# A two-layer image kernel on one core: the next image's transposes in one block, a mask built on GpSimd, a norm spread over three rows

## The chip, the cores and the metric

The kernel runs on one core of one Trainium2 chip. The metric is the device time of one execution in microseconds (us). In the traces PE is TensorE (PEld its weight loads), DVE is VectorE, ACT is ScalarE, POOL is GpSimd, and SP issues most DMAs.

## The reference: two residual layers on 32 images

The input is `x` of 32 images of 56 x 56 tokens with 128 channels, in fp32. Each layer normalises its input over 32 groups of channels and adds its result to it:

```python
x = x + L0(_gn(x), ...)   # shifted-window attention: windows of 7 x 7, shift 3, 4 heads
x = x + L1(_gn(x), ...)   # Fourier layer, then a feed-forward of 512
```

Layer 0 rolls the image by 3, cuts it into 8 x 8 windows of 49 tokens, computes q, k and v, adds to the scores a table of relative positions and a mask of -100 between tokens that were not neighbours before the roll, takes the softmax, and projects. The mask differs from zero only in the last row and the last column of windows. Layer 1 takes a cosine transform along each axis, keeps 32 modes, mixes the channels for each mode, transforms back, sums the two axes, and applies `relu(h @ W1 + b1) @ W2 + b2`.

## The kernel before

Work goes by **rows of windows**: 7 lines of an image, 8 windows. An image has 8 rows (`NWR`), and one turn of the main loop (line 1006), a *cycle*, does one row of attention and, some cycles behind, a share of the Fourier layer of an earlier image. The order of the instructions on PE, ACT, DVE and POOL is written by hand (`manual_schedule`, line 999): each of these engines works in program order. Slots of a tile's buffers are given out by a planner when the kernel is built. What lies ahead of line 999 (constants, masks) is ordered by that planner too.

**A cycle** from the 12th on (`CONV_BEGIN` = 11) sorts its matmuls by the part of the PE array that they use: `halves_first` (q and k, line 371; the first matmul of the feed-forward, line 738), for cycles without feed-forward `half_columns` (forward transforms, line 627, and mixing, line 670), then `eighths` (attention times values of three rows ago, line 487), `quarters` (scores, line 417, and the transforms back, line 706), `full` (transposes that use the whole array) and `halves_last` (v, line 400, the rest of the transforms, the feed-forward's second matmul, line 766, and the projection, line 534). Six names are used below: `attn_max` (line 445) is DVE's maximum and POOL's subtraction, `attn_exp` (line 453) ACT's exponential, `attn_divide` (line 457) DVE's sum and reciprocal and POOL's multiplication (called mult), `attn_transpose` (line 467) PE's transposes of the softmax, whose first half is copied out by DVE and second half by ACT (aT), and `attn_sums` (line 557) two DVE reductions and an ACT square for the second layer's norm, of which `fourier_stats` (line 579) makes the scale and shift.

**The first eleven cycles** run `first_rows` (line 956), which has attention alone.

**The next image.** `image_groups(im, i)` (line 267) turns rows i and i + 1 of an image into channels x tokens: 7 PE transposes into two PSUM banks (line 275), three ACT copies into `xw` (lines 287, 288 and 293), two POOL memsets, two DVE `bn_stats` (line 297), and on POOL the projection's bias added to `x` (line 306, two instructions). PSUM has eight banks of one tile each: four called pa (`attn_bank`) and four called pc (`conv_bank`). `next_groups` (line 916) calls it twice in row 5 and twice in row 6 of the image before (the first image: rows 4 and 5). `full` does the softmax's transposes only in even cycles, for two rows at once. `image_norm` (line 315) is a generator in steps: the DVE chain and POOL's power (lines 333 to 355), the scaled weights `wn` and the negated mean `nb` (lines 359 and 362), and a small PE product for v's bias (line 365). For the first image all steps run before row 0; for the second in row 6, one after another; for later ones in row 7.

**The mask.** `bias_and_mask(r)` (line 187) adds the table of positions and the mask into `bm` with 16 instructions of 49 x 98; r = 0 is for the rows 0 to 6 and is done before the rows begin, r = 1 for row 7, done on DVE at the end of row 1 (line 985). Its source `mask_sb` lies in the buffer of the tag sq, which `attn_sums` uses from row 4 on.

Which cycle has no feed-forward: cycles 11 to 18, and later every row 6 (`FF_AT`, line 43). The transforms back stand in the Fourier cycles 5 to 8 (`back_groups`, line 829), which are the cycles 16 to 19 for the first image and have feed-forward beside them for nearly all others.

Of the kernel before, what the change touches and what calls it, by code (L numbers as in the profile page):

```python
# [10 lines left out]
F32 = mybir.dt.float32  # L11
# [4 lines left out]
P = 128  # L16
# [32 lines left out]
def swin_fourier_kernel(  # L49
# [33 lines left out]
    def attn_bank():  # L83
        return bank("pa", 4)
# [87 lines left out]
            )  # L172
    nc.sync.dma_start(rpb[JP : JP + WT], rpb[0:WT])

    mask_sb = work.tile([P, 4, C], F32, tag="sq", name="mask", bufs=1).rearrange("p n c -> p (n c)")
    mask_sb = mask_sb[:, : 4 * WT].rearrange("p (r k j) -> p r k j", r=2, k=2)
    nc.vector.memset(mask_sb, 0.0)
    for hh in range(2):
# [5 lines left out]
    nc.gpsimd.memset(bm, 0.0)  # L184
    rpb_f = rpb.rearrange("p (t u) y x -> p t u (y x)", u=2)

    def bias_and_mask(r):
        for t in range(2):
            for half in range(2):
                rows = slice(half * JP, half * JP + WT)  # L190
                for k, p0, p1 in ((0, 0, NP - half), (1, NP - half, NP)):
                    for p in range(p0, p1):
                        nc.vector.tensor_tensor(
                            bm[rows, r, t, p],
                            rpb_f[rows, t],
                            mask_sb[rows, r, k].unsqueeze(1).to_broadcast([WT, 2, WT]),
                            ALU.add,
                        )

    bias_and_mask(0)  # L200
# [66 lines left out]
    def image_groups(im, i):  # L267


        pt = [attn_bank(), attn_bank()]  # L270
        pts = [
            p[:, : n * S].rearrange("p (j r s) -> p j r s", r=n, s=WS) for p, n in zip(pt, (8, 6))
        ]
        for c in range(7):
            nc.tensor.transpose(  # L275
                pts[c // 4][:, :, 2 * (c % 4) : 2 * (c % 4) + 2],
                im.x[:, WS * i // 2 + c],
                ident_x[:, :, SS:].rearrange("p r (j s) -> p j r s", s=WS),
            )
# [35 lines left out]
    def image_norm(im):  # L315
# [38 lines left out]
        rstd = small.tile([P, 1], F32, tag="rstd0", name="rstd0")  # L354
        nc.gpsimd.tensor_tensor(rstd, ve, mhalf, ALU.pow)
        im.w = work.tile([P, 3 * C], F32, tag="wn", name="wn")
        yield
        nb = small.tile([P, 1], F32, tag="nb0", name="nb0")
        nc.vector.scalar_tensor_tensor(
# [3 lines left out]
        yield  # L363
        pb = attn_bank()
        halved(pb[:, 0:1], wqkv[:, 2 * C :], nb)
        im.bias = small.tile([P, 5], F32, tag="bqkv", name="bqkv")
        nc.vector.tensor_copy(im.bias[:, 2:3], pb[:, 0:1])
        yield

# [451 lines left out]
    def row(r):  # L821
        return (images[r // NWR], r % NWR) if 0 <= r < NB * NWR else (None, 0)
# [17 lines left out]
    def nothing():  # L840
        while True:
            yield

    def load_first(cycle):
        for im, c in fourier(cycle):
            if c == 0:
                load_columns(im, 0)
                load_columns(im, 1)

    def halves_first(cycle, norm):  # L850
        for im, c in fourier(cycle):
            if c == 0:
                im.stats = fourier_stats(im)
                im.cols = {}
                next(im.stats)
        last, j = row(cycle - 4)
        sums = attn_sums(last, j) if last and cycle > CONV_BEGIN else nothing()
        next(sums)
        im, i = row(cycle)
        if im:  # L860
            attn_qk(im, i, False)
        next(norm)
        next(sums)
        for im, c in fourier(cycle):
            if c in FF_AT:
                ff_in(im, FF_AT.index(c))
        for im, c in fourier(cycle):
            if c == 0:
                next(im.stats)
# [21 lines left out]
                    mix(im, True, g)  # L891

    def quarters(cycle):
        im, i = row(cycle)
        if im:
            attn_scores(im, i, cycle)
        for im, c in fourier(cycle):
            for width, g in back_groups(c):
                modes_back(im, width, g)

    def eighths(cycle):
        im, i = row(cycle - 3)
# [13 lines left out]
    def next_groups(cycle):  # L916
        b, i = divmod(cycle, NWR)
        if b + 1 < NB:
            for j in {(4 if b == 0 else 5): (0, 2), (5 if b == 0 else 6): (4, 6)}.get(i, ()):
                image_groups(images[b + 1], j)  # L920

    def last_out(cycle):
# [4 lines left out]
    def halves_last(cycle, norm):  # L927
        im, i = row(cycle)
        if im:
            attn_v(im, i, cycle)  # L930
        if has_ff(cycle):
            half_columns(cycle)
        half_columns(cycle, True)
        load_back(cycle + 1)
        next_begin(cycle)
        load_first(cycle)
        next(norm)
        if row(cycle)[0]:
# [6 lines left out]
        next(norm)  # L945

    def next_begin(cycle):
        b, i = divmod(cycle, NWR)
# [7 lines left out]
    def first_rows(cycle, norm):  # L956
# [15 lines left out]
            attn_max(cycle)  # L972
        if im3:
            attn_project(im3, i3)
        next(norm)
        last, j = row(cycle - 4)
        if last:
            for _ in attn_sums(last, j):
# [7 lines left out]
        next(norm)  # L986
# [9 lines left out]
        next(norm)  # L996

    ET = mybir.EngineType
    with tc.manual_schedule(engines={ET.PE, ET.Activation, ET.DVE, ET.Pool}):
        images[0] = image_begin(0)  # L1000
        for i in range(0, NWR, 2):
            image_groups(images[0], i)
        for _ in image_norm(images[0]):
            pass
        norm = nothing()
        for cycle in range(NB * NWR + CONV_BEGIN + FF_AT[-1] - NWR + 1):
            if cycle < CONV_BEGIN:
                first_rows(cycle, norm)
            else:
# [10 lines left out]
                    half_columns(cycle)  # L1020
                eighths(cycle)
                quarters(cycle)
                if row(cycle)[0] and cycle % 2:
# [4 lines left out]
            norm = nothing()  # L1028
            if i == (NWR - 2 if b else NWR - 3) and b + 1 < NB:
                norm = image_norm(images[b + 1])  # L1030
                next(norm)


# [60 lines left out]
```

## Time and profile before

| | us |
|---|---|
| median of 3 runs | 3635.16 (3634.94 to 3637.57) |
| profiled execution | 3641.7 |
| its span, first to last instruction | 3639.9 |
| PE busy in the span | 3574.4 |
| DVE, ACT, POOL busy | 2211.9, 2148.1, 1368.3 |
| longest group: second feed-forward matmul (L112, pc<-wff,hid) | 740.3 for 12544, 273 ns each |
| transposes of L275 | 896, of 112x112 |
| POOL's subtract and multiply (L449, L463) | 389.4 and 389.1, 1521 and 1520 ns each |

A line of a timeline reads: start and duration in us from the span's start, engine, source line, operation, written tile <- read tiles, shape, count of merged instructions, and in brackets how long the engine was idle before and what ended that. Since matmuls overlap, the cost of a group on PE is read from its start to the start of the next group. The granted clock is the share of TensorE's full clock that the throttle allowed.

### The profile page before, as it was taken

What the parts mean: (1) busy time and instruction counts of PE and PEld (TensorE: products, weight loads), DVE (VectorE), ACT (ScalarE), POOL (GpSimd) and SP (SyncE); (2) the same over time, 40 slices, a digit from 0 to 9 for tenths busy, and PEclk for the clock granted to TensorE, in tenths of its full rate; (3) what the DMA queues carried; (4) which work ended last, traced back from release to release, by engine and by line L of the source; (5) the groups of instructions that cost most, each with busy time, mean ns of one, the idle gap of its engine ahead of it and who ended that gap; (6) DMA issues with size and microseconds to landing.
All of it is one profiled execution on the core that took longest, in us unless ns stands there. A gap on an engine that the chain in (4) does not pass through costs nothing.

```text
span 3639.9 us, 161666 instructions
## 1 busy us (share of the span) xinstructions
PE 3574.4 (98%) x72192; PEld 2832.6 (78%) x72192; DVE 2211.9 (61%) x4738; ACT 2148.1 (59%) x4044; POOL 1368.3 (38%) x1421
## 2 busy tenths in 40 slices
PE   7899999999999999999999999999999999999999
PEld 5677777778777787877777878777777777787776
DVE  7766666666666666666656656666566666565641
ACT  4555566655566555666556665556665556655553
POOL 5433333333343433333333434333333334343321
PEclk8999999999999999999999999999999999999999
DMA  4334434444434444334444344443444443444343
GB/s 114 86 102 112 113 96 111 108 110 111 112 97 112 112 109 116 94 110 107 113 108 111 94 114 109 113 114 94 111 108 111 110 111 94 114 109 109 97 115 98
DMA packets 687350, 390.31 MB, mean 107 GB/s; under 512 B 39967, under 2 KB 657600, under 8 KB 686400
## 3 DMA queue, kind: packets, MB, share of 16 engines
q1 hardware_dynamic: 686045, 379.65, 38.3%
q8 instruction: 568, 9.31, 1.1%
q14 instruction: 126, 1.03, 0.1%
q10 hardware_dynamic: 611, 0.32, 0.0%
HBM read 218.29 MB, written 161.48 MB: 104 GB/s over the span
## 4 chain that ended last, share of the span: by engine, by line
PE 92%; DVE 4%; issue 1%; ACT 1%; POOL 1%; DMA 1%; SPq 0%; POOLq 0%; DVEq 0%; ACTq 0%
PE pc L112 37%; PE pa L112 14%; PE pa L408 6%; PE pc L679 6%; PE pa L474 6%; PE pc L645 6%; PE pa L430 5%; PE pa L499 4%; PE pc L718 4%; PE pa L275 3%; DVE a L438 1%; DVE xf L729 0%; DVE oT L530 0%; POOL rstd L616 0%; ACT a L455 0%
## 5 line engine op out<-in xcount | busy, mean ns | idle before, releaser
L449 POOL TENSOR_TENSOR a<-a,mx 128x784 f32<-128x784 f32 x256 | 389.4, 1521 | 1427.3 <-DVE mx L448 1203.4
L112 PE MATMUL pc<-wff,hid 128*64 128x128 f32 x12544 | 740.3, 273 | 1.5 <-ACT hid L763 0.8
L112 PE MATMUL pc<-xf,wff 128*64 128x512 f32 (+2 forms) x3584 | 717.5, 539 | 1.1 <-DVE xf L729 1.0
L112 PEld LDWEIGHTS pc<-wff,hid 128*64 128x64 f32 x12544 | 702.6, 137 | 8.2 <-ACT hid L763 4.5
L460 DVE TENSOR_REDUCE sm<-a 128x16 f32<-128x784 f32 x256 | 248.2, 970 | 686.1 <-ACT a L455 682.8
L463 POOL TENSOR_TENSOR a<-a,rs 128x784 f32<-128x784 f32 x256 | 389.1, 1520 | 566.6 <-DVE rs L462 542.8
L763 ACT ACTIVATE hid<-pc,b1sb 128x512 f32<-128x512 f32 (+2 forms) x896 | 527.1, 632 | 76.6 <-PE pc L112 74.5
L112 PEld LDWEIGHTS pc<-xf,wff 128*64 128x64 f32 x3584 | 279.8, 137 | 368.0 <-issue 260.5
L379 ACT ACTIVATE q<-pa,bqkv 128x392 f32<-128x392 f32 x256 | 150.4, 587 | 473.1 <-PE pa L112 467.5
L112 PE MATMUL pa<-xw,wn 128*64 128x392 f32 (+1 forms) x2048 | 390.6, 497 | 3.7 <-DVE aT L484 2.7
L530 DVE TENSOR_SCALAR oT<-pa,bqkv 128x98 f32<-128x98 f32 (+2 forms) x768 | 171.0, 278 | 268.7 <-PE pa L499 268.6
L751 POOL TENSOR_TENSOR res<-res,b2sb 128x512 f32<-128x512 f32 (+2 forms) x256 | 264.2, 1037 | 113.5 <-DMA res<-scr 113.5
L408 PE MATMUL pa<-wn,xw 128*64 128x128 f32 x4096 | 283.6, 280 | 4.7 <-issue 3.5
L306 POOL TENSOR_TENSOR xl<-xl,bproj 112x512 f32<-112x512 f32 (+1 forms) x256 | 286.8, 1142 | 0.0
L499 PEld LDWEIGHTS pa<-aT,v 49*32 49x32 f32 x16384 | 172.9, 106 | 146.1 <-issue 127.0
L415 ACT COPY v<-pa 128x512 f32<-128x512 f32 x256 | 150.9, 589 | 228.3 <-PE pa L408 228.3
L438 DVE TENSOR_TENSOR a<-pa,bm 128x392 f32<-128x392 f32 x512 | 264.8, 559 | 25.8 <-PE pa L430 2.1
L455 ACT ACTIVATE a<-a 128x784 f32<-128x784 f32 x256 | 222.3, 869 | 97.2 <-POOL a L449 96.8
L482 ACT COPY aT<-pa 113x452 f32<-113x452 f32 x256 | 139.4, 544 | 210.4 <-PE pa L474 206.6
L408 PEld LDWEIGHTS pa<-wn,xw 128*64 128x64 f32 x4096 | 221.4, 137 | 38.6 <-issue 9.1
L112 PE MATMUL pa<-wproj,oT 128*64 128x128 f32 (+1 forms) x3584 | 248.0, 274 | 1.8 <-DVE oT L530 1.8
L448 DVE TENSOR_REDUCE mx<-a 128x16 f32<-128x784 f32 x256 | 246.3, 962 | 4.3
(91 smaller groups left out, 5583.8 us busy)
## 6 DMA issues: line engine op xcount, KB each, us to landing
zscr<-z SPq DMA_DIRECT2D x512, 112.0 KB
htok<-scr SPq DMA_DIRECT2D x256, 196.0 KB
zT<-zscr SPq DMA_DIRECT2D x192, 256.0 KB
res<-scr SPq DMA_DIRECT2D x160, 256.0 KB
out_dram<-res SPq DMA_DIRECT2D x160, 256.0 KB
scr<-xl SPq DMA_DIRECT2D x128, 224.0 KB
xl<-in_x_dram SPq DMA_DIRECT2D x32, 784.0 KB
xl<-in_x_dram SPq DMA_DIRECT2D x32, 672.0 KB
```

The lines of the kernel that those rows point to most:

```text
L112: nc.tensor.matmul(dst[ps], lhsT=lhsT[:, ps], rhs=rhs, start=start, stop=stop)
L306: nc.gpsimd.tensor_tensor(piece, piece, bproj.unsqueeze(1).to_broadcast([TC, e - a, C]), ALU.add)
L408: nc.tensor.matmul(pv[hs, j * C : (j + 1) * C], lhsT=im.xw[i][:, w * WT : w * WT + JP], rhs=im.w[:, 2 * C : 3 * C], start=True, stop=True,)
L438: nc.vector.tensor_tensor(a[:, 2 * hp : 2 * hp + 2, :, 0:WT].rearrange("p u w j -> p w u j"), ps[hp][:, :RT].rearrange("p (w u j) -> p w u ...
L448: nc.vector.tensor_reduce(mx, a3, axis=AX.X, op=ALU.max)
L449: nc.gpsimd.tensor_tensor(a3, a3, mx.unsqueeze(2).to_broadcast([P, 2 * NWR, WT]), ALU.subtract)
L455: nc.scalar.activation(a3, a3, AF.Exp)
L460: nc.vector.tensor_reduce(sm, a3, axis=AX.X, op=ALU.add)
L463: nc.gpsimd.tensor_tensor(a3, a3, rs.unsqueeze(2).to_broadcast([P, 2 * NWR, WT]), ALU.mult)
L499: nc.tensor.matmul(po4[u][h * HD : (h + 1) * HD, 2 * f + e], lhsT=v[ks, 2 * f + e, h * HD : (h + 1) * HD], rhs=im.aT[i][f][ks, h, e * JP : ...
L751: nc.gpsimd.tensor_tensor(res[:m, c0:c1], res[:m, c0:c1], b2sb[:m].unsqueeze(1).to_broadcast([m, c1 - c0, C]), ALU.add,)
L763: nc.scalar.activation(hf[:, :n], ph[:, :n], AF.Relu, bias=b1sb[:, f : f + 1])
```

## The change

- `next_groups`: from the second image on, all four calls for the next image stand in row 6, and row 5 has none. For the first image nothing moves.
- `image_groups`: the calls for i = 2 and 6 take their two PSUM banks from pc instead of pa.
- The mask: `mask_sb` moves to the tag res (first used by the feed-forward in cycle 19). `bias_and_mask` takes the engine and does a quarter of the work at a call; the table for row 7 is built on GpSimd, half (8 instructions) in cycle 4 and half in cycle 5, ahead of that cycle's `next_groups`.
- The norm: the generator goes on over cycles instead of being thrown away at the end of each. The first image's runs up to `wn` before row 0, and its small product comes in row 0. The second image's steps come in rows 6, 7 and 8 of the loop. Later images have the first two steps in row 7 and the product in the next row's `halves_first`. In a cycle without feed-forward the step stands after `quarters`.
- `quarters`: in cycles without feed-forward the transforms back come ahead of the scores.
- `first_rows`, last turn (cycle 10): the first image's Fourier statistics begin here, and the last row's sums come ahead of exponential and division; before, the statistics began in cycle 11 and the sums came behind.

```diff
-    mask_sb = work.tile([P, 4, C], F32, tag="sq", name="mask", bufs=1).rearrange("p n c -> p (n c)")
+    mask_sb = work.tile([P, 4, C], F32, tag="res", name="mask").rearrange("p n c -> p (n c)")
...
+    def bias_and_mask(engine, r, t, half):
+        rows = slice(half * JP, half * JP + WT)
+        for k, p0, p1 in ((0, 0, NP - half), (1, NP - half, NP)):
+            for p in range(p0, p1):
+                engine.tensor_tensor(
+                    bm[rows, r, t, p],
...
+    for t in range(2):
+        for half in range(2):
+            bias_and_mask(nc.vector, 0, t, half)
...
-        pt = [attn_bank(), attn_bank()]
+        pt = [conv_bank() if i % 4 else attn_bank() for _ in range(2)]
...
+    def start_stats(im):
+        im.stats = fourier_stats(im)
+        im.cols = {}
+        next(im.stats)
...
     def halves_first(cycle, norm):
         for im, c in fourier(cycle):
-            if c == 0:
-                im.stats = fourier_stats(im)
-                im.cols = {}
-                next(im.stats)
+            if c == 0 and cycle > CONV_BEGIN:
+                start_stats(im)
...
-        next(norm)
+        if has_ff(cycle):
+            next(norm, None)
...
     def quarters(cycle):
+        def back():
+            for im, c in fourier(cycle):
+                for width, g in back_groups(c):
+                    modes_back(im, width, g)
+
+        if not has_ff(cycle):
+            back()
         im, i = row(cycle)
         if im:
             attn_scores(im, i, cycle)
-        for im, c in fourier(cycle):
-            for width, g in back_groups(c):
-                modes_back(im, width, g)
+        if has_ff(cycle):
+            back()
...
-            for j in {(4 if b == 0 else 5): (0, 2), (5 if b == 0 else 6): (4, 6)}.get(i, ()):
+            for j in ({4: (0, 2), 5: (4, 6)} if b == 0 else {6: (0, 2, 4, 6)}).get(i, ()):
                 image_groups(images[b + 1], j)
...
-        if cycle == 1:
-            bias_and_mask(1)
-        next(norm)
+        if cycle in (4, 5):
+            for half in range(2):
+                bias_and_mask(nc.gpsimd, 1, cycle - 4, half)
...
         if cycle == CONV_BEGIN - 1:
+            start_stats(im3)
+            for _ in attn_sums(im3, i3):
+                pass
             attn_exp(cycle)
             attn_divide(cycle)
-            for _ in attn_sums(im3, i3):
-                pass
...
-        for _ in image_norm(images[0]):
-            pass
-        norm = nothing()
+        norm = image_norm(images[0])
+        for _ in range(3):
+            next(norm)
...
                 eighths(cycle)
                 quarters(cycle)
+                if not has_ff(cycle):
+                    next(norm, None)
```

`halves_last` loses its last `next(norm)`, `first_rows` two of its three, and the line that reset `norm` in each cycle goes.

More of the change, by code (lines that the diff above doesn't have):

```diff
@@ L185, in swin_fourier_kernel @@
     rpb_f = rpb.rearrange("p (t u) y x -> p t u (y x)", u=2)
[L187 to L200, printed above, removed]
+    def bias_and_mask(engine, r, t, half):
[4 more added lines that the diff above has]
+                    bm[rows, r, t, p],
+                    rpb_f[rows, t],
+                    mask_sb[rows, r, k].unsqueeze(1).to_broadcast([WT, 2, WT]),
+                    ALU.add,
+                )
+    for t in range(2):
+        for half in range(2):
+            bias_and_mask(nc.vector, 0, t, half)
     dct_w = const_load([TC, 2 * NM], dct, "dct_w")
@@ L356, in image_norm @@
         im.w = work.tile([P, 3 * C], F32, tag="wn", name="wn")
+        im.bias = small.tile([P, 5], F32, tag="bqkv", name="bqkv")
         yield
@@ L365, in image_norm @@
         halved(pb[:, 0:1], wqkv[:, 2 * C :], nb)
-        im.bias = small.tile([P, 5], F32, tag="bqkv", name="bqkv")
         nc.vector.tensor_copy(im.bias[:, 2:3], pb[:, 0:1])
@@ L944, in halves_last @@
             attn_project(im, j)
-        next(norm)
     def next_begin(cycle):
@@ L974, in first_rows @@
             attn_project(im3, i3)
-        next(norm)
+        next(norm, None)
         last, j = row(cycle - 4)
@@ L983, in first_rows @@
             image_bias(im, 2 * cycle)
-        if cycle == 1:
-            bias_and_mask(1)
-        next(norm)
+        if cycle in (4, 5):
+            for half in range(2):
+                bias_and_mask(nc.gpsimd, 1, cycle - 4, half)
         next_begin(cycle)
@@ L989, in first_rows @@
         if cycle == CONV_BEGIN - 1:
+            start_stats(im3)
+            for _ in attn_sums(im3, i3):
+                pass
             attn_exp(cycle)
             attn_divide(cycle)
-            for _ in attn_sums(im3, i3):
-                pass
             last, j = row(cycle - 1)
             attn_transpose(last, j, cycle - 1)
-        next(norm)
     ET = mybir.EngineType
@@ L1022, in swin_fourier_kernel @@
                 quarters(cycle)
+                if not has_ff(cycle):
+                    next(norm, None)
                 if row(cycle)[0] and cycle % 2:
@@ L1027, in swin_fourier_kernel @@
             b, i = divmod(cycle, NWR)
-            norm = nothing()
             if i == (NWR - 2 if b else NWR - 3) and b + 1 < NB:
                 norm = image_norm(images[b + 1])
-                next(norm)
+                next(norm, None)
 def _constants():
```

## The prediction

> **What bounds the kernel now.** I read the page first: busy shares, then the chain that ended last. Its columns are the engine, busy us, share of the span and instruction count; the chain gives shares of the span by engine.
>
> ```profile
> span 3639.9 us, 161666 instructions
> PE 3574.4 (98%) x72192; PEld 2832.6 (78%) x72192; DVE 2211.9 (61%) x4738; ACT 2148.1 (59%) x4044; POOL 1368.3 (38%) x1421
> PE 92%; DVE 4%; issue 1%; ACT 1%; POOL 1%; DMA 1%; SPq 0%; POOLq 0%; DVEq 0%; ACTq 0%
> ```
>
> PE is busy 98% of the span and carries 92% of the chain. So time goes only if PE gets fewer or shorter instructions, or if one of its rare waits goes. The page's second part puts those waits at the start: PE's first two slices (of 91 us) read 7 and 8, all later ones 9. Next, what PE waits for (total us, times, longest):
>
> ```profile
> engine line waited for: us in total, times, longest us
> PE pa L112 <- DVE nb L359: 10.3, 3, 4.7
> PE pc L718 <- issue: 4.3, 8, 0.8
> PE pa L112 <- DVE tot L581: 4.0, 1, 4.0
> PE pa L112 <- DVE aT L484: 2.7, 1, 2.7
> ```
>
> The norm (nb), the second norm's sums (tot) and a late eviction (aT) are all one-time waits before 170 us, and the diff touches the work in front of each.
>
> **Steady state: one block of transposes.** PE's timeline in a middle image (start, duration, engine, line, count) shows rows 5 and 6:
>
> ```profile
> 791.79 0.91 PE L430 MATMUL pa<-k,q 64*64 64x98 f32 x32
> 792.63 1.72 PE L275 MATMUL pa<-ident_x,xl 112*128 112x112 f32 x14
> 794.28 1.09 PE L408 MATMUL pa<-wn,xw 128*64 128x128 f32 x16
> ...
> 805.73 1.85 PE L474 MATMUL pa<-ident,a 113*113 113x113 f32 x16
> 807.41 1.98 PE L275 MATMUL pa<-ident_x,xl 112*128 112x112 f32 x14
> 809.32 1.09 PE L408 MATMUL pa<-wn,xw 128*64 128x128 f32 x16
> ```
>
> Start to start, the 14 transposes cost 794.28 - 792.63 = 1.65 us in row 5 and 809.32 - 807.41 = 1.91 us in row 6: 3.56 us an image. Who is waited for at L275 explains most of the difference:
>
> ```profile
> L275 PEld LDWEIGHTS pa<-ident_x,xl x896: 137/139/231, 6.9 to 3369.4; 112*128 112x128 f32 x180
>   DVE aT L484: 7.6, 29
> ```
>
> That is 0.26 us an image: the second call of row 6 needs a bank that DVE's aT copy leaves at 808.82.
>
> Afterwards row 6 runs 28 transposes behind the 16 of L474. The rate comes from L474: 807.41 - 805.73 = 1.68 us for 16, 0.105 each, entry included. Leaving the full array costs 0.09 (in row 8 of that stretch 16 of L474 and the exit take 835.95 - 834.18 = 1.77). So 28 x 0.105 + 0.09 = 3.03 us: 0.53 saved. The calls now alternate between the banks pa and pc, so the first reuse of the late aT bank comes a call later, at 807.41 + 14 x 0.105 = 808.88, just after 808.82: that wait should go. If it stays, 0.27 is left. The row-4 and row-5 runs of image 0 took 1.62 for 14 (0.115 each), which gives 0.25 to 0.5. I take 0.45, for 30 images (the second image's transposes stay in rows 4 and 5): **13.5 us** (8 to 16).
>
> What follows the block must not be late. ACT copies two calls in 1.81 us (808.06 to 809.87), so four end at 811.7, v, two z copies and exp(6) follow, and q of row 7 starts near 815.0, when PE (qk at 812.87 + 1.3) has its first half. DVE does eight bn_stats at 0.49 each from 808.73 to 812.7 and then waits for exp as now. POOL has four bias pairs and memsets of 2.35 us behind the subtract that ends at 809.94: free at 819.4, 4.4 after mult(6) now starts (815.05), but the transposes that read it come at 834.18. Its pow (819.29 now) slips to about 821.5, before ACT starts wn at 822.70. PE wants q only at its scores (818.45), wn at 826.19, mult(6) at 834.18: each is covered by some 3 us or more.
>
> **Start, the mask.** DVE's 16 mask adds of row 1 take 6.23 us (33.69 to 39.92) ahead of aT; PE waits 2.68 us for that copy at 40.63. With them gone aT is done by 35, and what is late next is the row's own score add, near 38.8, for the second half of qk: 2.5 us go. The wait also left the granted clock at 0.61 from 40.63 to 49.40; against rows at 1.00 the five groups there (1.04, 1.86, 1.61, 1.54, 1.35 against 0.81, 1.39, 1.41, 0.87, 1.04) lose 1.9; I credit half. **3.4 us** (0.5 to 4.5). The moved bias product shifts the banks of rows 0 and 1: 0.7 either way, inside that range.
>
> **Start, the norm and what GpSimd then does.** PE ends row 6 at 72.71 and waits for nb:
>
> ```profile
> 71.67 1.04 PE L408 MATMUL pa<-wn,xw 128*64 128x128 f32 x16
> 77.12 0.38 PE L112 MATMUL pa<-nb,wqkv 128*64 128x1 f32 x4 [4.41 <-DVE nb L359]
> 77.33 2.89 PE L112 MATMUL pa<-xw,wn 128*64 128x392 f32 x8
> ```
>
> Row 7 takes 86.92 - 72.71 = 14.2 us where row 9 takes 100.19 - 93.80 = 6.4: 4.41 of wait and the rest a clock of 0.64. Spread over three rows, nb is ready a row ahead of its product, so 7.8 us could go. But the masks stand in GpSimd's queue in rows 4 and 5, in front of the biases, and GpSimd is nearly full there:
>
> ```profile
> 60.34 2.23 POOL L306 TENSOR_TENSOR xl<-xl,bproj 112x512 f32<-112x512 f32 x2
> 63.24 1.52 POOL L463 TENSOR_TENSOR a<-a,rs 128x784 f32<-128x784 f32 x1 [0.67 <-DVE a L438]
> 64.79 1.52 POOL L449 TENSOR_TENSOR a<-a,mx 128x784 f32<-128x784 f32 x1
> 71.05 1.52 POOL L463 TENSOR_TENSOR a<-a,rs 128x784 f32<-128x784 f32 x1 [0.17 <-DVE rs L462]
> ```
>
> No row has a 49x98 add on POOL. Below it stands the 128x15 memset (111 ns), above it the 64x128 add of L751 (448 ns). The add is the nearer in kind; back to back, two L306 of 1.28 us end in 2.23, so an instruction hides 0.3 of its neighbour's overhead at most, and I take 0.3: 2.5 us a row (0.9 to 3.6). Followed through: biases of row 4 end at 65.1 (now 62.57), mult(4) 66.6, subtract 68.1, mask 70.6, biases 75.2, mult(5) 76.7, subtract(6) 78.2. PE would want mult(5) at 72.71 + 1.43 + 0.74 = 74.9: a new wait of 1.8. Behind subtract(6), ACT does exp and then oT (to 79.5), which the projection needs: row 7 ends near 82.2 instead of the ideal 79.1. Of 7.8 us 3.1 are given back: **4.5 us** (1 at 0.45 us an add, 7.5 at 0.11).
>
> One row speaks against the move as well: while POOL ran a subtract of 1.57 us in row 1, one of DVE's mask adds lasted 1572 ns (L193: minimum 245, median 253), so the two engines block each other there. The Trainium skill, "GPSIMD Engine Reference", section 8, says that GpSimd contends with DVE instructions that have two SBUF inputs; section 4.1 counts two-input elementwise work about twice as slow on GpSimd, which agrees with 1277 ns for L751 beside 680 for DVE's L787 of the same size. By that an add would cost twice DVE's 253 ns, 4 us a row, the norm's gain would be near zero and the sum some 20.
>
> **Start, second norm.** PE waits 3.97 us until 113.39 for tot, behind sum, reciprocal, two sums and aT on DVE. Moved ahead of exp, tot is done at 109.2 and the last sum (after ACT's square) near 110.5; exp itself ends at 109.7 either way, and sum(10) slips by 0.8, mult(10) to 113.3, needed two rows later. What is late next is the sum, or the bank of the aT copy (now 112.7): 2.9 or 1.1 go. **2.5 us** (0.5 to 4, with the clock of 0.86 there).
>
> **Transforms ahead of scores.** This moves work only in rows 16 to 18. There PE waits 0.39, 1.90 and 1.70 for k of L396. But scores lead to add, max, subtract, exp, q, k and the next k in a ring (182.52 to 191.22, 8.7 us) that a fuller wait doesn't shorten; only row 18's end gains, where scores' add then also stands behind 2 us of xf adds. **0.5 us** (-1 to 2.5). The norm step of row 15 stands after the scores instead of before: the stall on oT (1.79) goes, and one on wn takes its place (add ends 162.9, eleven small ones 2.4, pow and wn 0.6 each: 166.6 against qk at 166.29): 0 (-1.5 to 1.5). No DMA moves past another, except that the mask's tile now lies in the res buffers, which ff_in first takes in row 19.
>
> **Sum.** 13.5 + 3.4 + 4.5 + 2.5 + 0.5 = 24.4 us of the profiled execution's 3641.7 (span 3639.9 and 1.8 around it). The runs' median is 3635.16, 0.18% below that execution; the same difference gives 3610.8.
>
> **Rivals.** A: GpSimd eats the start's gain (0.45 us an add or more, and the waits cool the clock). For it: 0.17 us of slack before mult(5). Against: rows 6 to 8 have POOL idle to catch up. Only the block and a little remain: -15, 3620. B: the block saves nothing, since the two pc banks or the aT banks stall it as at 808.56 now; only the start remains: -11, 3624. C, slower: the bank that v of row 6 takes is one that ACT drains last. The block would end at 810.5 and ACT at 811.7, so PE waits 1.2 us in 30 images: 36 - 24.4 = 11.6 slower, 3647. It decides from 24.4 / 30 = 0.81 us an image. Against it: v, projection and qk need four pa banks only over 3.6 us, and a call's first bank is free early.
>
> **How the numbers follow.** Forecast 0.60, A 0.17, B 0.15, C 0.08. A measurement of this kernel tells about 0.2% (7.3 us) from no change. Faster: 0.60 + 0.17 and half of B, 0.84; same, the rest of B and a part of C, 0.10; slower 0.06. The range takes in the bounds of the start and reaches to A and B: 3602 to 3625.
>
> **What would show it.** Right: no L275 in row 5, 28 in row 6 within 3.0 to 3.2 us, no wait of L275 on aT; no wait of PE on nb or 2.7 on aT; mult(5) as a new wait of L474 near 75. Wrong: v or qk of rows 6 and 7 waiting for ACT xw (C), an L275 block of over 3.4 us (B), or POOL adds over 0.45 us (A).

## The result and the profile after

The changed kernel takes 3614.53 us (median of 4 runs, 3612.19 to 3617.05) beside 3636.36 for the kernel before on the same chip (3634.94 to 3638.27): a ratio of 0.994 with an interval of 0.9923 to 0.9957, or 21.8 us less. The forecast was 3610.8 in a range of 3602 to 3625. The profiled execution took 3612.19, with a span of 3610.4.

The page of the changed kernel (busy us, share, count; then the chain's shares) has PE as busy as before, on 21.1 us less of work:

```profile
span 3610.4 us, 161666 instructions
PE 3553.3 (98%) x72192; PEld 2827.3 (78%) x72192; DVE 2256.6 (63%) x4722; ACT 2145.8 (59%) x4044; POOL 1375.3 (38%) x1437
PE 93%; DVE 4%; ACT 1%; issue 1%; POOL 1%; DMA 0%; SPq 0%; ACTq 0%; POOLq 0%; DVEq 0%
```

What PE waits for (total us, times, longest) shows which one-time waits have gone and what stands in their place. Source lines above L200 are one or two higher than in the kernel before:

```profile
engine line waited for: us in total, times, longest us
PE pa L112 <- ACT wn L364: 8.3, 2, 5.1
...
PE pa L475 <- POOL a L464: 3.8, 2, 3.4
...
PE pa L431 <- DVE oT L531: 1.1, 1, 1.1
```

The waits on nb (10.3), tot (4.0) and aT (2.7) are gone. The 5.1 on wn is the first image's own start (4.7 on nb before), the other 3.3 of wn is the third image's norm at 159.05. A wait for GpSimd's multiplication (L464) of 3.4 is new, and so is one of 1.1 for DVE's oT.

**The block.** PE's timeline of the same place in the same image (start, duration, ..., count) has one run of 28 transposes, on the two tags in turn:

```profile
794.26 1.85 PE L475 MATMUL pa<-ident,a 113*113 113x113 f32 x16
795.95 0.92 PE L276 MATMUL pa<-ident_x,xl 112*128 112x112 f32 x7
796.71 0.88 PE L276 MATMUL pc<-ident_x,xl 112*128 112x112 f32 x7
797.42 0.87 PE L276 MATMUL pa<-ident_x,xl 112*128 112x112 f32 x7
798.13 0.87 PE L276 MATMUL pc<-ident_x,xl 112*128 112x112 f32 x7
798.93 1.09 PE L409 MATMUL pa<-wn,xw 128*64 128x128 f32 x16
```

798.93 - 795.95 = 2.98 us, where rows 5 and 6 took 3.56 together. What these transposes still wait for is only the start-up's input, no aT:

```profile
its engine sat idle before it (us, times) until:
  DMA xl<-in_x_dram: 8.0, 3
  DVE ident_x L144: 6.6, 1
  issue: 0.3, 2
```

The shortest time from one image's first qk matmul to the next one's fell with it from 110.70 to 110.11.

**Row starts.** The rest is read from the start of each row's first qk matmul in PE's timeline (us from the span's start). The kernels e1 to e10 are the experiments below.

| kernel | row 0 | 4 | 6 | 8 | 11 | 12 | 17 | 20 | 24 |
|---|---|---|---|---|---|---|---|---|---|
| before | 18.4 | 49.4 | 65.9 | 86.9 | 107.9 | 121.8 | 178.1 | 216.7 | 271.9 |
| after | 17.9 | 44.7 | 61.1 | 81.8 | 103.2 | 114.2 | 171.1 | 208.9 | 263.4 |
| e1 block alone | 18.2 | 48.8 | 65.5 | 84.8 | 105.7 | 120.2 | 178.0 | 217.3 | 271.8 |
| e2 all but the block | 18.1 | 46.1 | 63.1 | 83.3 | 104.7 | 116.3 | 170.7 | 208.8 | 263.8 |
| e3 mask on DVE | 18.8 | 51.1 | 67.5 | 81.7 | 103.7 | 114.7 | 171.8 | 209.8 | 264.2 |
| e4 biases late | 18.9 | 45.6 | 62.0 | 78.3 | 100.5 | 114.8 | 171.1 | 209.0 | 263.4 |
| e5 block, pa only | 18.8 | 45.5 | 62.0 | 82.6 | 104.3 | 116.7 | 170.5 | 208.2 | 263.0 |
| e6 norm in row 6 | 19.0 | 46.7 | 63.4 | 88.9 | 109.9 | 120.9 | 177.7 | 215.8 | 270.2 |
| e7 scores first | 18.3 | 48.0 | 64.4 | 85.1 | 106.5 | 117.5 | 174.3 | 214.0 | 268.4 |
| e8 late biases, early norm | 18.2 | 46.4 | 62.9 | 77.9 | 100.0 | 111.0 | 168.6 | 206.5 | 261.0 |
| e9 biases beside the norm | 18.5 | 46.9 | 63.9 | 81.9 | 103.6 | 114.6 | 172.6 | 210.8 | 265.3 |
| e10 sums behind exp | 18.6 | 47.1 | 63.5 | 84.2 | 105.6 | 119.5 | 177.0 | 215.0 | 269.4 |

From row 0 to row 4 the same code takes 26.7 to 29.7 us from one execution to another, so a kernel is read by differences between rows, and a term of the first rows only to a microsecond or two.

The profiled spans differ by 29.5 us: 8.5 are there at row 24; 28 images at 0.59 give 16.5; the last rows 0.6; and 4.0 is chance. What the 28 images take beyond 28 times the shortest one sums to 15.1 us before and to 11.1 after (12.7 to 16.3 in the experiments), mostly waits named "issue", in front of which the profile shows nothing. So the medians' 21.8 is the better measure of the whole. For the block alone the profiles give a better one: from row 24 to row 248 the nine executions with the whole block take 3094.3 to 3099.6 us (3097.8 on average), the two without it 3114.7 and 3112.0. That is 15.5 us for 28 images, 0.55 an image.

**The norm's rows.** From row 6 to row 8 the kernel takes 20.7 us, as long as before (21.0). PE's timeline of the changed kernel's row 7:

```profile
67.29 1.49 PE L112 MATMUL pa<-xw,wn 128*64 128x392 f32 x8
68.71 0.81 PE L500 MATMUL pa<-aT,v 49*32 49x49 f32 x64
72.92 1.86 PE L475 MATMUL pa<-ident,a 113*113 113x113 f32 x8 [3.41 <-POOL a L464]
75.63 0.59 PE L431 MATMUL pa<-k,q 64*64 64x98 f32 x4 [0.85 <-ACT oT L533]
77.30 1.57 PE L431 MATMUL pa<-k,q 64*64 64x98 f32 x28 [1.08 <-DVE oT L531]
78.80 1.54 PE L112 MATMUL pa<-wproj,oT 128*64 128x128 f32 x12
80.12 1.90 PE L409 MATMUL pa<-wn,xw 128*64 128x128 f32 x16
81.82 1.51 PE L112 MATMUL pa<-xw,wn 128*64 128x393 f32 x8
```

Three waits, and behind the first a slow clock (1.86 for eight transposes, 1.90 for v's sixteen matmuls that take 1.04 in row 6). The table by stretch gives the granted clock in the column behind POOL's busy time:

```profile
core 0: us, PE busy (x) PEld busy (x) DVE busy (x) ACT busy (x) POOL busy (x), PEclk, DMA share, GB/s
...
67.30:81.80 14.50, 9.17 (x144) 7.28 (x142) 13.98 (x26) 5.16 (x9) 9.96 (x11) 0.65 0.13 36
```

POOL just ahead of that stretch and in it is the predicted queue: masks, biases, then the multiplication that PE waits for, and the subtraction of row 7:

```profile
63.66 2.94 POOL L191 TENSOR_TENSOR bm<-rpb,mask 49x98 f32<-49x98 f32 x8
66.66 0.15 POOL L284 MEMSET xw<- 128x15 f32 x2
66.89 2.25 POOL L307 TENSOR_TENSOR xl<-xl,bproj 112x512 f32<-112x512 f32 x2
69.06 0.16 POOL L284 MEMSET xw<- 128x15 f32 x2
69.17 2.23 POOL L307 TENSOR_TENSOR xl<-xl,bproj 112x512 f32<-112x512 f32 x2
71.34 1.53 POOL L464 TENSOR_TENSOR a<-a,rs 128x784 f32<-128x784 f32 x1
72.82 1.52 POOL L450 TENSOR_TENSOR a<-a,mx 128x784 f32<-128x784 f32 x1
```

And DVE beside it shows what the forecast did not have:

```profile
69.21 0.19 DVE L322 TENSOR_REDUCE gsums<-turned 128x8 f32<-128x32 f32 x1
69.44 3.47 DVE L325 TENSOR_SCALAR gmeans<-gsums 128x32 f32<-128x32 f32 x1
72.94 1.45 DVE L340 TENSOR_TENSOR turned<-turned,gmeans 128x32 f32<-128x32 f32 x1
...
76.50 0.66 DVE L531 TENSOR_SCALAR oT<-pa,bqkv 128x98 f32<-128x98 f32 x3
```

L325 works on 32 numbers a partition; at 74.87, with POOL idle, the same instruction takes 0.18 us. Here it ends at 72.91, when POOL's multiplication ends (72.87), and L340 ends at 74.39 with POOL's subtraction (74.34). So the tiny instructions of the norm waited for GpSimd, and behind them in DVE's order oT, for which PE waits at 77.30.

The same happens in nearly every later image, where the block has moved GpSimd's bias additions beside the norm. All instructions of three lines in the whole execution (count, then shortest, median and longest in ns):

```profile
L322 DVE TENSOR_REDUCE gsums<-turned x64: 185/186/188, 14.6 to 3351.4; 128x8 f32<-128x32 f32 x64
L325 DVE TENSOR_SCALAR gmeans<-gsums x64: 180/182/3470, 14.8 to 3351.7; 128x32 f32<-128x32 f32 x64
L340 DVE TENSOR_TENSOR turned<-turned,gmeans x32: 193/1451/1457, 15.0 to 3349.7; 128x32 f32<-128x32 f32 x32
```

30 of the 32 L340 take 1.45 us and end 0.04 to 0.05 after a GpSimd instruction; before the change none took over 0.19. It is the block that brings them together: the median of this instruction is 1.45 in e1, with the block alone, and 0.19 in e2, without it. 30 of the 64 L325 and 30 of the 64 L322 start while GpSimd works: each of those L325 is held, and no L322 is. Only in the second image's row 7 does PE wait for what stands behind them.

### The profile page after: what moved, and what is told of

Read it like the earlier page. It is cut to its first block, busy times and chain, and to the rows that moved or that the text cites. A ratio compares the mean times of both kernels' runs of the same rounds, so it can differ in the third digit from the quotient of the medians.

```text
span 3610.4 us, 161666 instructions
## 1 busy us (share of the span) xinstructions
PE 3553.3 (98%) x72192; PEld 2827.3 (78%) x72192; DVE 2256.6 (63%) x4722; ACT 2145.8 (59%) x4044; POOL 1375.3 (38%) x1437
## 4 chain that ended last, share of the span: by engine, by line
PE 93%; DVE 4%; ACT 1%; issue 1%; POOL 1%; DMA 0%; SPq 0%; ACTq 0%; POOLq 0%; DVEq 0%
PE pc L112 38%; PE pa L112 15%; PE pa L409 6%; PE pc L680 6%; PE pa L475 6%; PE pc L646 6%; PE pa L431 5%; PE pa L500 4%; PE pc L719 4%; PE pa L276 1%; PE pc L276 1%; DVE a L439 1%; DVE xf L730 0%; DVE oT L531 0%; POOL rstd L617 0%
## 5 line engine op out<-in xcount | busy, mean ns | idle before, releaser
L464 POOL TENSOR_TENSOR a<-a,rs 128x784 f32<-128x784 f32 x256 | 389.7, 1522 | 609.1 <-DVE rs L463 553.8
L531 DVE TENSOR_SCALAR oT<-pa,bqkv 128x98 f32<-128x98 f32 (+2 forms) x768 | 171.1, 278 | 242.5 <-PE pa L500 242.4
L307 POOL TENSOR_TENSOR xl<-xl,bproj 112x512 f32<-112x512 f32 (+1 forms) x256 | 287.5, 1146 | 0.1
L500 PEld LDWEIGHTS pa<-aT,v 49*32 49x32 f32 x16384 | 172.3, 105 | 145.6 <-issue 119.5
L475 PE MATMUL pa<-ident,a 113*113 113x113 f32 x2048 | 242.9, 271 | 7.1 <-POOL a L464 3.8
```

The lines of the kernel that those rows point to most:

```text
L307: nc.gpsimd.tensor_tensor(piece, piece, bproj.unsqueeze(1).to_broadcast([TC, e - a, C]), ALU.add)
L464: nc.gpsimd.tensor_tensor(a3, a3, rs.unsqueeze(2).to_broadcast([P, 2 * NWR, WT]), ALU.mult)
L475: nc.tensor.transpose(pt[:PW, h * P : h * P + PW], a[:PW, h, 2 * hf : 2 * hf + 2].rearrange("p w j -> p (w j)")[:, :PW], ident[:PW, :PW],)
L500: nc.tensor.matmul(po4[u][h * HD : (h + 1) * HD, 2 * f + e], lhsT=v[ks, 2 * f + e, h * HD : (h + 1) * HD], rhs=im.aT[i][f][ks, h, e * JP : ...
```

## The experiments

"The changed kernel" is the one after the change. Ratios are to the kernel before on the same chip.

**e1: the block alone.** The kernel before with the two edits of the block:

```diff
-        pt = [attn_bank(), attn_bank()]
+        pt = [conv_bank() if i % 4 else attn_bank() for _ in range(2)]
...
-            for j in {(4 if b == 0 else 5): (0, 2), (5 if b == 0 else 6): (4, 6)}.get(i, ()):
+            for j in ({4: (0, 2), 5: (4, 6)} if b == 0 else {6: (0, 2, 4, 6)}).get(i, ()):
```

> The kernel before with one part of the change alone: the next image's four transpose calls in row 6, every second one in the pc banks. Theory (the block is worth 0.58 us in each of 30 images and touches nothing else): the shortest period of an image on PE is 110.1 us instead of 110.7, the first rows keep their times of before (row 8 starts at 86.9), and the total is 17 us below before (15 to 19). Rival (part of the steady gain needs the norm step that moved behind the next row's q and k): the period is 110.3 or more and the total less than 12 us below.

Measured: 3627.47 beside 3639.77, ratio 0.9965 (0.9953 to 0.9978), so 12.3 us less (8 to 17). The shortest image takes 110.11, as in the changed kernel; row 17 starts at 178.0, as before. So the period has the block's 0.59 an image, with nothing else changed, and from row 24 to row 248 this execution takes 15.3 less than the kernel before. The total is below the 15 to 19 that were named; this profile's excess over the shortest images is the largest of all, 16.3.

**e2: all but the block.** The changed kernel with those two edits undone.

> The changed kernel with the transposes back in rows 5 and 6 and in the pa banks only, so that mask, norm, statistics and the order of the transforms remain. Theory: the period is 110.7 us again, row 8 starts at 81.8 and row 12 at 114.2 as in the changed kernel, and the total is 8 us below before (6 to 10). Rival (the block's four calls in row 14 cost the start some of its gain): the start gains over 10 us.

Measured: 3629.09, ratio 0.9968 (0.9957 to 0.998), so 10.7 us less; shortest image 110.69, row 17 at 170.7. The total is over the 6 to 10 that were named, but the rows do not bear out the rival: at row 20 this kernel is 7.9 ahead of the one before and the changed kernel 7.8. The two halves add up: 12.3 + 10.7 = 23.0, beside 21.8 for both.

**e5: the block on pa alone.** The changed kernel with the first of the two edits undone, so that the 28 transposes stand in one run but no bank comes from pc:

> The changed kernel with all four transpose calls of an image in the four pa banks; pc is not used. Theory (half of the block's gain comes from the banks: calls in pa reach the late aT bank 0.7 us earlier and later calls wait for ACT's copies): the 28 transposes take 3.3 to 3.6 us instead of 2.99, with the waits on DVE aT and ACT xw back, the shortest period is 110.4 to 110.7 and the total 8 to 17 us above the changed kernel. Rival (the gain is only that of leaving the full array once less): 3.0 to 3.1 us, period 110.1 to 110.2, total within 3 us of the changed kernel.

Measured: 3625.74 beside 3638.11, ratio 0.9964 (0.9951 to 0.9978); shortest image 110.47. The transposes take 801.77 - 798.44 = 3.33 us, and who is waited for at L276 has the late copy back (and ACT's xw once, for 1.1):

```profile
its engine sat idle before it (us, times) until:
  DMA xl<-in_x_dram: 8.0, 2
  DVE aT L485: 7.9, 30
```

So of the 0.59 an image 0.36 belong to the two pc banks (7.9 / 30 = 0.26 of it the named wait) and 0.23 to the merging of the two rows.

**e3: the mask on DVE again.** The changed kernel with the second table built in row 1, as before:

```diff
-        if cycle in (4, 5):
-            for half in range(2):
-                bias_and_mask(nc.gpsimd, 1, cycle - 4, half)
+        if cycle == 1:
+            for t in range(2):
+                for half in range(2):
+                    bias_and_mask(nc.vector, 1, t, half)
```

> The changed kernel with the last row's mask back on VectorE in row 1, the rest as changed. Theory (GpSimd's queue, with the mask in rows 4 and 5, is what eats the norm's gain): row 3 starts some 4 us later than in the changed kernel (40.1), but the wait of the transposes in row 7 for mult shrinks from 3.4 us to under 0.5 and row 7 takes 6.5 to 7.5 us instead of 14.5, so row 8 starts at 78 to 79 instead of 81.8: 3 us faster than the changed kernel. Rival (row 7 is held by the second image's norm and its biases, whatever the mask does): row 7 still takes over 12 us, row 8 starts at 85 to 86, and the kernel is 4 us slower than the changed one.

Measured: 3614.38 beside 3639.77, ratio 0.9931 (0.9917 to 0.9944). PE waits 2.68 for aT at 41.34 again and row 4 starts at 51.1; but the wait for L464 is gone, L325 lasts 0.25, and rows 6 to 8 take 14.2 instead of 20.7. Row 8 starts at 81.7, the changed kernel's at 81.8, and at row 24 both are 245.5 us behind row 0. So row 7 went as the theory said, and the 3 us in total did not come. The masks on GpSimd are what took the norm's gain (by GpSimd's queue or by the hold on DVE, which this run does not tell apart), and their move, taken alone, is worth nothing to within the scatter of the first rows: what it saves ahead of row 4 it costs in rows 6 and 7.

**e4: the biases later.** The changed kernel with the second image's eight additions of L307 not in rows 4 and 5 but a pair each at the end of rows 7 to 10:

```diff
-        if im.b:
+        if im.b > 1:
             image_bias(im, i)
...
+        if cycle >= CONV_BEGIN - 4:
+            image_bias(images[1], 2 * (cycle - CONV_BEGIN + 4))
```

> The changed kernel with the second image's four bias additions on GpSimd moved from rows 4 and 5 to the ends of rows 7 to 10, where GpSimd has some 3 us free in each; the mask stays on GpSimd in rows 4 and 5. Theory (GpSimd is full in rows 4 to 6, and any 2 us off it will do): no wait for mult in row 7, row 7 takes 6.5 us, row 8 starts at 74 and the total is 7 to 8 us below the changed kernel. Rival (the DVE work of row 6, sums and norm together, is next late): row 7 takes 9 to 11 us and the gain is 3 to 5 us.

Measured: 3612.83 beside 3639.77, ratio 0.9926 (0.9914 to 0.9939). No wait for L464; row 7 lasts 10.1, as the rival had it. PE's waits in it are now those for oT, which stands behind the norm's eleven small instructions in DVE's order:

```profile
72.23 0.39 PE L431 MATMUL pa<-k,q 64*64 64x98 f32 x4 [0.45 <-ACT oT L533]
73.78 1.57 PE L431 MATMUL pa<-k,q 64*64 64x98 f32 x28 [1.16 <-DVE oT L531]
```

So with the queue cleared DVE is next: rows 6 to 8 take 16.3, a gain of 4.5 over the changed kernel. It isn't kept. Row 11 lasts 14.3 instead of 11.0, since v waits 3.18 for ACT's oT at 111.77. Row 12, without a stop of 2.19 that the changed kernel has there, gives 3.7 back; rows 13 to 16 take 46.6 instead of 43.6, and at row 17 both kernels start at 171.1. The wait in row 11 is the last bias pair's: it runs on GpSimd from 105.98, the power of the second norm (L617) starts behind it at 108.17, ACT waits 4.56 for that until 108.75 and only then comes to oT, at 111.29. A DVE instruction of the same norm (L613, 128x1, two inputs) takes 1.18 beside the pair instead of 0.16. In e8, which has no pair in row 10, the power starts at 105.85 and row 11 lasts 11.0.

**e9: the biases beside the norm.** As e4, but each pair in rows 6 to 9 directly behind POOL's subtraction, so that in row 6 it runs just when the norm's small instructions do:

```diff
             attn_max(cycle)
+        if NWR - 2 <= cycle < NWR + 2:
+            image_bias(images[1], 2 * (cycle - NWR + 2))
```

> As the late biases, but in rows 6 to 9 and directly behind the subtraction, so that in row 6 GpSimd's 2.2 us of bias additions run beside the norm's small DVE instructions while nothing that PE waits for is queued behind them. It tells GpSimd's queue from a block of DVE by GpSimd. Block (GpSimd's additions hold up a DVE instruction that reads two SBUF operands or runs in a fast mode, as the 3.47 us of one 32-element L325 in the changed kernel suggest): one small DVE instruction of the norm in row 6 lasts 1.5 to 3 us, DVE's oT of row 7 comes 2 us later than with the late biases alone, and row 8 starts at 80 to 81 instead of 78.3. Queue alone: no small DVE instruction over 0.3 us there, and row 8 starts at 78.3 as before.

Measured: 3616.93 beside 3638.11 (one run). POOL and DVE in row 6:

```profile
70.95 1.52 POOL L450 TENSOR_TENSOR a<-a,mx 128x784 f32<-128x784 f32 x1 [0.38 <-DVE mx L449]
72.43 2.22 POOL L307 TENSOR_TENSOR xl<-xl,bproj 112x512 f32<-112x512 f32 x2
72.25 0.26 DVE L325 TENSOR_SCALAR gmeans<-gsums 128x32 f32<-128x32 f32 x1
72.54 1.21 DVE L340 TENSOR_TENSOR turned<-turned,gmeans 128x32 f32<-128x32 f32 x1
73.79 0.92 DVE L341 TENSOR_TENSOR turned<-turned 128x32 f32<-128x32 f32 x1
74.74 0.19 DVE L322 TENSOR_REDUCE gsums<-turned 128x8 f32<-128x32 f32 x1
```

L325 meets the end of POOL's subtraction (72.47), here as in e4, and takes 0.26 instead of 0.18. L340 and L341, 0.19 each in e4, are held, each until one L307 ends. The chain is 1.75 us longer, PE waits 2.91 for DVE's oT instead of 1.16, and rows 6 to 8 take 18.0 instead of e4's 16.3. Two instructions share the delay that the theory had put on one. The same instructions with and without GpSimd beside them: that GpSimd holds up these instructions of DVE is shown.

**e6: the norm in one row again.** The changed kernel with the second image's remaining norm steps also at the end of row 6:

```diff
+        if cycle == NWR - 2:
+            for _ in range(2):
+                next(norm, None)
```

> The changed kernel with the second image's norm all in row 6, as before the change; the mask stays on GpSimd. Theory (in the changed kernel rows 6 and 7 are held by GpSimd's queue and by the norm's DVE chain, which GpSimd's long run stretches, so that the wait on nb was only one of several that overlap): PE's wait on nb is back at the end of row 6, 8 to 9 us long, since the DVE chain ends only at 75.6; the wait for mult is gone in exchange, and row 8 starts at 84 to 86 instead of 81.8. Rival (the spread norm is worth its whole 7.8 us): row 8 starts at 89 or later. Second rival (worth nothing): row 8 at 81 to 82.5.

Measured: 3622.80 beside 3638.11 (one run). nb is waited for again, longer than before the change, since the chain is now held by GpSimd (L325 takes 3.42 us and L340 1.45):

```profile
79.10 0.38 PE L112 MATMUL pa<-nb,wqkv 128*64 128x1 f32 x4 [9.28 <-DVE nb L361]
```

Row 8 starts at 88.9, of which 2.4 were there at row 6. Rows 6 to 8 take 25.5: the spread over three rows is worth 4.7 us there, but beside masks on GpSimd it only repairs what these cost.

**e10: the sums behind the exponential.** The changed kernel with the last turn of the first rows and the start of the statistics as before:

```diff
-            if c == 0 and cycle > CONV_BEGIN:
+            if c == 0:
...
-            start_stats(im3)
-            for _ in attn_sums(im3, i3):
-                pass
             attn_exp(cycle)
             attn_divide(cycle)
+            for _ in attn_sums(im3, i3):
+                pass
```

> The changed kernel with one part undone: in the last turn of the first rows the statistics begin a cycle later again and the last row's sums stand behind exponential and division. Read by row starts of the profile, not by the whole time. My theory (the sums that stand ahead of the exponential carry the term of 2.5): the wait on tot comes back with 3 to 4 us and rows 11 to 12 last 2 to 3.5 us longer than in the changed kernel, so row 12 starts 116.2 to 117.7 instead of 114.15; none of it is given back before row 17. Rival (tot was late only because the rows before it were): the wait is under 1.5 us and row 12 starts before 115.5.

Measured: 3623.51 beside 3645.74 for the kernel before on that chip (one run of each). The wait is back, for 3.98 us,

```profile
111.08 0.34 PE L112 MATMUL pa<-tot,gmean 112*64 112x64 f32 x4 [3.98 <-DVE tot L582]
```

and row 11 lasts 14.0 instead of 11.0. All rows of this execution had started later (row 11 by 2.4), which is why its row 12 lies beyond the window that was named; the difference of 3.0 between the rows is inside it. From row 12 to row 17 the two take 57.4 and 56.9, so nothing is given back.

**e7: scores first.** The changed kernel with the transforms back behind the scores in all cycles:

```diff
-        if not has_ff(cycle):
-            back()
         im, i = row(cycle)
...
-        if has_ff(cycle):
-            back()
+        back()
```

> The changed kernel with one part undone: the transforms back stand behind the scores in every cycle, those without feed-forward too, as before. Read by row starts of the profile. My theory (the ring from scores over softmax to k sets these rows, and the order of the transforms inside it does not): row 19 starts within 0 to 1.5 us of the changed kernel's 190.63, and waits for k of 0.4 to 2 us are there in both. Rival (the order is worth its place): row 19 starts 2 to 4 us later than in the changed kernel.

Measured: 3621.29 beside 3645.74 (one run of each). Row 19 starts at 195.0, but 3.3 of that were there at row 11, and rows 11 to 16 differ by more than the order's effect between kernels that have the same code there. Rows 17 and 18 don't: together they take 20.7 here, in the kernel before and in e1, and 19.5 to 19.6 in the eight kernels with the new order (19.9 in e8, whose third norm is moved too). So the order is worth 1.1 us, inside the theory's window, but it isn't nothing: all of it lies in row 17, where the transforms now fill the wait for k, 1.90 here at 178.67 and 0.58 in the changed kernel at 175.44. In row 18 the waits only change their names (1.70 for k here; 2.12 for q and 1.85 for DVE's scores there). Row 19 is another 0.7 longer here than in the changed kernel, but it varies by as much between the others (18.0 to 18.7).

**e8: late biases and an early norm.** As e4 with the pairs at the ends of rows 6 to 9; and the third image's first norm step stands in row 14 right behind its transposes, to take away the 3.3 us of wait for wn:

```diff
+        if NWR - 2 <= cycle < NWR + 2:
+            image_bias(images[1], 2 * (cycle - NWR + 2))
...
                 full(cycle)
+                early = cycle == 2 * NWR - 2
+                if early:
+                    norm = image_norm(images[2])
+                    for _ in range(2):
+                        next(norm)
-                halves_last(cycle, norm)
+                halves_last(cycle, nothing() if early else norm)
+                if early:
+                    continue
```

> The changed kernel with two moves: the second image's bias additions on GpSimd at the ends of rows 6 to 9 (behind the norm's power), and the third image's first norm step in row 14, right behind its transposes, where DVE waits 2.2 us for the exponential. Theory: row 8 starts near 78.3 and row 11 at 100 as with the late biases alone; row 11 loses nothing to a late power on GpSimd, so row 12 starts at 111; the 3.3 us wait for wn before row 16 goes, and row 17 starts at 164 to 166 instead of 171: 5 to 7 us below the changed kernel. Rival (rows 12 to 17 are held by the ring from scores to the next k, whatever comes earlier): row 17 starts at 169 to 171 and the total is within 2 us of the changed kernel.

Measured: 3611.57 beside 3638.11 (3610.96 to 3615.82), ratio 0.9926 (0.9913 to 0.994). Rows 6 to 8 take 15.0, row 12 starts at 111.0 and keeps e4's gain. The wait for wn is gone, but its place is taken:

```profile
154.18 1.16 PE L431 MATMUL pa<-k,q 64*64 64x98 f32 x32 [3.35 <-DVE k L397]
```

and row 17 starts at 168.6, 2.5 us before the changed kernel's and not the five or more that were hoped for. That lies between theory and rival. It is the lowest median of all; its interval overlaps the changed kernel's, so that it is faster than that one is likely from the row starts and not shown by the times.

## Why the prediction was right, point by point

The sum was 24.4 us and 21.8 were measured. That they lie so near is in part luck: the block gave some 3 us more than its term, and the norm's term, which failed, some 4 less. The terms as measured below add up to some 24 us again, which the result's interval (15.6 to 28.0) holds. The terms, each with what it became:

- **PE is the bound, and the block is the largest term.** Right. 0.45 an image were taken. The block itself measures 0.58, the shortest period 0.59 and the average from row 24 to row 248 0.55: some 17 us for 30 images (an estimate from these) instead of 13.5. The totals alone, 12.3 in e1, would not show that it was more. The terms of the working were better than the value chosen from them: 0.53 from the exit and the entry with the wait gone, and that wait did go (e5 has it back).
- **What follows the block has cover.** Right: ACT copies the four calls from 796.60 to 800.07, 4.1 us behind the block's start (4.3 forecast), q of the next row starts 7.4 behind it (7.6 forecast), and v, qk and projection wait for no bank there. Rivals B and C fell with this.
- **The mask, 3.4.** From row 0 to row 4 the nine kernels with this code take 27.9 us on average, before and e1 30.8 (e3, also with the mask on DVE, 32.4): 2.9, from executions that differ by as much among themselves. The granted clock from row 3 to row 4 is 1.00, where it was 0.61. The suspected shift of banks is there (row 0 is 2.1 longer, row 1 2.1 shorter) and cancels.
- **The norm, 4.5: the step that failed.** Rows 6 to 8 gained 0.3. The 7.8 that the spread over three rows could give were nearly right: e3, with the masks off GpSimd, takes 6.9 less there than the kernel before. What was mis-sized is what GpSimd takes back: 3.1 in the forecast, 6.6 measured (20.7 in the changed kernel, 14.2 in e3). The prediction followed POOL's queue: "PE would want mult(5) at 72.71 + 1.43 + 0.74 = 74.9: a new wait of 1.8", and oT at 79.5. The wait came, at the same place, and was 3.41. The additions took 0.34 and 0.37 us each (2.68 and 2.94 for eight) instead of 0.30, and PE came 5.4 us earlier than the working had it (69.5 instead of 74.9), GpSimd's multiplication only 3.8 (72.9 instead of 76.7). What had no term at all is the other direction of the block between GpSimd and DVE. The prediction had the row that showed it (an addition of DVE's held for 1572 ns in row 1) and used it only against the price of the mask additions; that the norm's own chain would run on DVE beside a GpSimd without a gap, and hold oT, was not followed. The Trainium skill has it: "SBUF — State Buffer", section "SBUF: two separate sides", calls the pair of ports that the two share an exclusive lock, which the one that starts first keeps for the whole instruction; there is a condition that the DVE instruction has two SBUF inputs or runs in a mode with two ports. e9 agrees for a DVE instruction that comes second: the two-input L340 and L341 waited for one POOL instruction each. No run here shows one that came first. That L325, with one tensor input, is held as well, while L322, also with one, never is, fits only the second kind; that L325 runs in such a mode no run here shows.
- **The second norm, 2.5.** Right: 3.0 in e10, 2.9 from the kernel before to the kernel after.
- **Transforms ahead of scores, 0.5; the third image's norm, 0.** e7 gives 1.1 for the first, in row 17 and not at the end of row 18, where the working had it: the wait for k isn't merely moved, the transforms fill it. For the second, the forecast's exchange of an oT wait for one on wn came about ("166.6 against qk at 166.29" was a wait of 0.3 on wn; it is 3.26). Row 15 takes 9.86 us, before 9.88, so the exchange is worth nothing, as forecast, though the wait itself was mis-sized.

So the start gave 7.8 at row 20 instead of 10.9, and the block gave more. Of the rivals, A (GpSimd eats the start's gain) came half true: the masks at 0.37 are below its 0.45, but with the hold on DVE they cost as much in rows 6 and 7, as e3 shows.

**Open.** Rows 11 to 17 take more or less time from kernel to kernel by up to 4 us in ways that these runs do not sort out: of e4's gain of 4.5 in rows 6 and 7 nothing is left at row 17, and e8's gain of 3.3 in front of row 16 is lost in row 15. In row 12 PE stops for some 2 us (2.19 in the changed kernel, at 119.97) between two values matmuls with the name "issue". The stop is 0.9 in e1, 0.3 in e5 and not there in e4; nothing in the profile says what it waits for.

## What to carry to other kernels

Where one engine is busy nearly all the time, a small saving in the block that comes once per image is worth more than the repair of long waits that come once: 0.55 to 0.59 us an image became some 17. Banks from a second tag are 0.36 of it, so look at who frees the bank that a longer block takes next. Before work moves from DVE to GpSimd because GpSimd is idle on average, look at its queue in just those rows and at which small DVE instructions will stand beside it: what the mask's move saved ahead of row 4 it took back in rows 6 and 7.

## What the runs showed of the hardware that was not expected

- A DVE instruction of 0.18 to 0.19 us lasted 3.47, 1.45, 1.21 and 0.92 us beside GpSimd additions and multiplications, and ended within 0.1 us of the end of one of them. One of 128x1 (nb, L361) took 1.29 us both in the changed kernel and in e4, each time until POOL's subtraction of 1.52 ended. L340 (128x32, two inputs) took 1.45 in 30 of the changed kernel's 32 images and 0.19 in all 32 before it.
- On GpSimd an addition of 49x98 takes 0.34 to 0.37 us back to back, beside DVE's 0.25.
- PE stops now and then for 0.2 to 1.5 us without anything in the profile that it waits for, 6.6 us after 380 us in the changed kernel's execution and 9.4 in the one before. Of ten executions of the kernel before on one chip the longest took 7.2 us more than the shortest (3636.82 to 3644.01).
